# Moving large matmul units between the two layers' steps in a two-layer graph attention kernel

## The chip, the cores and the metric

The kernel runs on one core of a Trainium2 chip. The metric is the device time of one execution in microseconds (us); lower is better. Engines are named as in the profile: PE is TensorE's matmuls and PEld its weight loads, DVE is VectorE, ACT is ScalarE, POOL is GpSimd, and SP is SyncE, which here only issues DMAs.

## The reference

For each of 16 graphs with 1024 nodes and 256 features, two attention layers follow each other. Both use the same adjacency matrix as a mask. Layer 0 has 4 heads of 64, layer 1 has 8 heads of 32 and biases on its projections.

```python
def layer(x, adj, H):                       # D = 256 // H
    h = maximum(layernorm(x), 0)
    q, k, v = heads(h @ Wq), heads(h @ Wk), heads(h @ Wv)
    s = where(adj != 0, q @ k.T / sqrt(D), -inf)
    return x + concat(softmax(s, -1) @ v) @ Wo + bo
x = layer(x, adj, 4)                        # layer 0, for each of the 16 graphs
x = layer(x, adj, 8)                        # layer 1
```

## The kernel before

**Tiles and steps.** A layer of one graph is cut into query halves (`qh`, 512 queries each) and, in each half, two groups of heads (`g`), so four groups a layer. A group runs through the keys in steps. One step computes 4 score blocks of 128 keys x 512 queries (`scores`, L396, into two PSUM tiles `ps` of two banks), masks them on DVE (L412), takes exponentials on ACT (L417) into a tile `p`, and two steps later (`LEAD = 2`) multiplies them with the values (`weigh`, L429, into `po`). A layer-0 step holds 2 heads x 2 key tiles, a group has 4 steps and a graph's layer 0 has 16. A layer-1 step holds 4 heads x 1 key tile, a group has 8 steps and a graph's layer 1 has 32.

**The order.** All 768 steps are in one list that is written out by hand: layer 0 of graph 0, then, for every b from 0 to 14, layer 0 of graph b+1 (16 steps, the first is called a) and layer 1 of graph b (32 steps, the first is called c = a + 16), and last layer 1 of graph 15. This text calls the 48 steps from a(b) on *period b*, and names steps a+0 to a+15 and c+0 to c+31; c+32 is the next period's a. Each engine works off its instructions in the order of the program.

**What hangs on the steps.** `later(i, f)` puts f on step i, behind the step's masks and exponentials. The *large units* are `k`, `q` and `values` (a projection of half a graph: 8, 8 and 16 PE instructions) and `end_half` (the output projection of half a graph, L377, 16 instructions). Each takes one PSUM tile from the same three as the scores. When a large unit is due on an even step, that step's `weigh` is put off and done on the following odd step together with its own (`Stream.run`). So the work goes in *pairs* of an even and an odd step, and a pair without a large unit is a *plain pair*. `turn` transposes a normalized half on PE (8 instructions) into a tile `hT`, of which there are two. For b from 1 on, the inputs of layer 1 of graph b (`mine` in the code) are made in the period itself or just ahead of it, those of layer 0 of graph b+2 (`other`) in c+1 to c+30.

**The softmax's sums.** In layer 1, POOL adds the p tiles of two steps (L530), and three accumulating DMAs of 1 MB a group (L516, POOL's queue) add the pairs' sums; one matmul with ones (`count`, L301) then gives the sums. In layer 0, DVE and POOL add the tiles (`add_tiles`, L438 to L444). `spread` copies the sums on ACT and sends them with 2 or 4 small DMAs on SP to `sums`, so that all lanes hold a part. `invert` takes the reciprocal on DVE (L337), writes it to DRAM (`vd`) and reads it back broadcast (`inv`, 2 or 4 DMAs; SP waits for `vd` to land). `normalize` multiplies `cat`, the group's output, on POOL (L348). `end_group` sets the distances: a group whose last `weigh` is done on step i has them, in layer 1, at i + 8, i + 11 and i + 15, and `end_half` at i + 17. The last group of a layer 1 is `brief` (4, 7, 9, 11) and the groups of graph 15's layer 1 are counted in `pairs`.

**Others.** `put` (ACT, L143) and `second` (DVE, L151, eight operations for a graph) make the mask; layer 1 needs `second`'s form. `norms` hangs statistics (DVE, L173) and the normalization (ACT, L190) on steps. `test` compares a layer's sums with two bounds (L247: two DVE instructions for layer 0, four for layer 1) and multiplies into `chk`, which `verdict` reduces at the end (L737), behind all output DMAs. After the last step `run` works off what is still due.

Of the kernel before, what the change touches and what calls it, by code (L numbers as in the profile page):

```python
# [10 lines left out]
F32 = mybir.dt.float32  # L11
# [7 lines left out]
P = 128  # L19
# [63 lines left out]
def fast_program(ctx, tc, a, w, loads, chk):  # L83
# [4 lines left out]
    x, adj, out = a["x"], a["adj"], a["out"]  # L88
    B, N, E = x.shape
    NT = N // P  # L90
# [3 lines left out]
    adjp = ctx.enter_context(tc.tile_pool(name="adjp", bufs=1))  # L94
# [3 lines left out]
    small = ctx.enter_context(tc.tile_pool(name="small", bufs=2))  # L98
# [173 lines left out]
    class Group:  # L272
# [44 lines left out]
        def spread(self):  # L317

            s = work.tile([P, 512], F32, tag="s", bufs=1, name=f"s_{self.n}")
            nc.scalar.copy(s, self.s)  # L320
            inp, k = self.inp, 2 * self.qh + self.g
            if k == 0:
                inp.sums = small.tile(
                    [P, 4 * self.n_f], F32, tag=f"sums{self.layer}", bufs=1, name=f"sums_{inp.n}"
                )
            self.sn = inp.sums[:, k * self.n_f : (k + 1) * self.n_f]
            lanes = P // self.per
            for r in range(self.per):
                nc.sync.dma_start(
                    self.sn[r * lanes : (r + 1) * lanes, :],  # L330
                    s[r * self.D : r * self.D + 1, :].rearrange("r (c f) -> r c f", f=self.n_f),
                )
# [122 lines left out]
    class Stream:  # L455
# [12 lines left out]
        def later(self, i, f, *args):  # L468
            self.due.setdefault(i, []).append((f, args))
# [84 lines left out]
        def end_group(self, i, gr):  # L554

            if gr.hurry:
                for f in (gr.spread, gr.finish, gr.inp.test):
                    self.later(i, f)
                return

            if gr.layer == 0:
                self.later(i + 4, gr.count_added)
                at = 4, 6, 8, 11
            else:
                at = (8, 11, 15, 17)
                if gr.pairs:
                    at = 2, 5, 7, 9
                elif gr.brief:
                    at = 4, 7, 9, 11
            for k, f in zip(at, (gr.spread, gr.invert, gr.normalize)):  # L570
                self.later(i + k, f)
            if gr.last:

                self.later(i + (7 if gr.layer or gr.inp.b == 0 else 37), gr.inp.test)
            if gr.g == 1:
                self.later(i + at[3], gr.end_half)

# [7 lines left out]
    mask, inp = masks[0], inputs[0][0]  # L585
# [76 lines left out]
    def norms(inp, half, *at):  # L662

        for i, f in zip(at, (inp.stats, inp.stats, inp.norm, inp.norm)):
            later(i, f, half, (0, 1) if i in (at[0], at[2]) else (2, 3))
        later(at[3] + 1, inp.add_bias, half)

    def half_inputs(inp, half, *at):

        for i, f in zip(at, (inp.turn, inp.k, inp.q, inp.values)):  # L670
            later(i, f, half)
# [5 lines left out]
    for t in range(NT):  # L677
        i = 6 + 2 * t
# [8 lines left out]
    for b in range(B - 1):  # L687
        mine, a, c = inputs[1][b], first[b + 1], second[b]
        if b == 0:

            norms(mine, 0, a + 5, a + 6, a + 8, a + 9)
            half_inputs(mine, 0, a + 11, a + 12, a + 14, a + 14)
            norms(mine, 1, a + 13, a + 14, a + 15, c)
            half_inputs(mine, 1, c + 1, c + 3, c + 6, c + 4)
        else:
            norms(mine, 0, a - 20, a - 19, a - 16, a - 15)
            half_inputs(mine, 0, a - 13, a, a + 4, a + 6)
            norms(mine, 1, a - 14, a - 10, a - 8, a - 6)
            half_inputs(mine, 1, a - 1, a + 8, c, a + 10)
        for i, u in zip((2, 4, 6, 8, 10, 11, 12, 14), range(NT)):  # L700
            later(a + i, masks[b].second, u)
        if b + 2 < B:
            other, mask = inputs[0][b + 2], masks[b + 2]
            later(a + 3, open_x, b + 2, 0)
            later(a + 13, open_x, b + 2, 1)
            if b == 0:
                norms(other, 0, a + 14, a + 15, c + 2, c + 3)
                half_inputs(other, 0, c + 5, c + 8, c + 16, c + 18)
                norms(other, 1, c + 3, c + 4, c + 6, c + 7)
                half_inputs(other, 1, c + 11, c + 22, c + 26, c + 30)  # L710
            else:
                norms(other, 0, a + 10, a + 12, a + 13, a + 15)
                half_inputs(other, 0, c + 1, c + 8, c + 16, c + 18)
                norms(other, 1, c, c + 4, c + 5, c + 6)
                half_inputs(other, 1, c + 9, c + 22, c + 26, c + 30)
            for i, t in zip((7, 12, 17, 22, 33, 37, 41, 45), range(NT)):
                later(a + i - 5 + (t > 4), mask.load, t)
                later(a + i - 2, mask.flip, t)
                later(a + i, mask.put, t)
        else:  # L720
            last, e = inputs[1][b + 1], c + 32
            norms(last, 0, c + 5, c + 6, c + 8, c + 9)
            half_inputs(last, 0, c + 11, c + 14, c + 16, c + 20)
            norms(last, 1, c + 13, c + 14, c + 16, c + 17)
            half_inputs(last, 1, c + 19, c + 24, e + 6, e + 4)
            for u in range(NT):
                later(c + 8 + 2 * u, masks[b + 1].second, u)
# [158 lines left out]
def kernel(  # L886
# [28 lines left out]
    with ExitStack() as fast, tc.manual_schedule():  # L915
        fast_program(fast, tc, a, w, loads, chk)
# [61 lines left out]
```

## Time and profile before

| | |
|---|---|
| median of 3 runs | 3368.06 us (3367.02 to 3372.03) |
| profiled execution, its own time | 3370.14 us |
| its span, first to last instruction | 3368.4 us |
| busy share of PE, PEld, DVE, ACT, POOL | 98, 38, 75, 64, 70% |
| granted TensorE clock | 0.989 |
| DMA queues, share of 16 engines | 37.0% from POOL, 13.5% from SP |

The busy time of PE includes waits inside a group of matmuls, since the ends of matmuls are modelled. More can be read from the starts of the score matmuls (L396), of which every step has one group: the distance between the starts of two even steps is what a pair takes. In period 5, which starts at 1153.65 us, the pairs take these times (from the timeline of PE; *L* marks a pair with a large unit):

| pair | us | pair | us | pair | us |
|---|---|---|---|---|---|
| a+0 L | 10.18 | c+0 L | 11.24 | c+16 L | 8.76 |
| a+2 L | 11.07 | c+2 | 4.50 | c+18 L | 8.67 |
| a+4 L | 13.76 | c+4 L | 9.24 | c+20 | 4.50 |
| a+6 L | 11.07 | c+6 | 4.51 | c+22 L | 8.00 |
| a+8 L | 11.91 | c+8 L | 9.33 | c+24 | 5.37 |
| a+10 L | 11.07 | c+10 | 4.50 | c+26 L | 7.69 |
| a+12 L | 11.93 | c+12 L | 8.36 | c+28 | 6.09 |
| a+14 | 7.57 | c+14 | 5.13 | c+30 L | 9.52 |

Pairs differ also by what else they hold: a `turn` (1.03 us of PE) or a `count` (0.9 to 2.7 us). Layer 0's pairs are the same in all of the periods 1 to 13; most of layer 1's are, but c+12, c+26 and c+28 vary.

### The profile page before, as it was taken

To read this page: it belongs to the slowest core of one execution; us is meant where nothing else is said; L and a number is where in the kernel's file an instruction comes from. 1 tells how busy PE (TensorE), PEld (TensorE's weight loads), DVE (VectorE), ACT (ScalarE), POOL (GpSimd) and SP (SyncE) were. 2 spreads that over 40 slices of the span, in tenths; PEclk is the share of its full clock that TensorE was granted. 3 is DMA by queue.
4 is the path that set the end of the run, shared out by engine and by line. 5 is a ranking of instruction groups with operands and counts; after the bars stand their busy time and mean duration, and the time that the engine had idled before them with its cause. 6 is when DMAs were issued, how large, how long until landed. Compare 5 with 4: busy or idle time off the path is not lost.

```text
span 3368.4 us, 44431 instructions
## 1 busy us (share of the span) xinstructions
PE 3293.8 (98%) x16990; PEld 1295.9 (38%) x16990; DVE 2528.6 (75%) x2760; ACT 2170.8 (64%) x2402; POOL 2344.8 (70%) x1244
## 2 busy tenths in 40 slices
PE   8999999999999999999999999999999999999898
PEld 3343433433343343433434333343333433433333
DVE  5777786878767787786877768778687776867876
ACT  6567576675756757576675766757567575675565
POOL 4578585775957759587684866848678585775675
PEclk9999999999999999999999999999999999999899
DMA  7348274472734727356282563826548274470431
GB/s 141 67 76 154 54 132 93 88 148 54 147 74 92 144 51 148 73 115 125 59 149 68 107 123 64 165 56 123 98 83 147 57 133 91 92 138 20 97 67 31
DMA packets 309454, 331.75 MB, mean 98 GB/s; under 512 B 189552, under 2 KB 257392, under 8 KB 290032
## 3 DMA queue, kind: packets, MB, share of 16 engines
q0 software_dynamic: 73824, 224.42, 37.0%
q1 hardware_dynamic: 235408, 104.41, 13.5%
q8 instruction: 135, 2.21, 0.3%
q14 instruction: 87, 0.71, 0.1%
HBM read 119.54 MB, written 17.56 MB: 41 GB/s over the span
## 4 chain that ended last, share of the span: by engine, by line
PE 70%; DMA 9%; POOL 9%; DVE 6%; issue 3%; SPq 2%; ACT 2%; POOLq 0%; DVEq 0%; ACTq 0%
PE ps L396 23%; PE po L429 20%; PE pq L225 9%; PE py L377 7%; POOL p L530 6%; PE pv L262 6%; DVE p L412 4%; PE pz L301 4%; DMA inv<-vd 3%; DMA vd<-vn 2%; DMA p<-p 2%; PE ph L208 1%; SPq L342 1%; ACT p L417 1%; POOL p L516 1%
## 5 line engine op out<-in xcount | busy, mean ns | idle before, releaser
L412 DVE SCALAR_TENSOR_TENSOR p<-mask,ps 128x1024 f32<-128x1024 fp8e4 x1536 | 1791.9, 1214 | 629.9 <-PE ps L396 572.4
L417 ACT ACTIVATE p<-p 128x1024 f32<-128x1024 f32 x1536 | 1610.7, 1056 | 926.4 <-DVE p L412 881.9
L530 POOL TENSOR_TENSOR p<-p,p 128x2048 f32<-128x2048 f32 x255 | 1210.1, 4748 | 154.2 <-PE po L429 135.0
L396 PE MATMUL ps<-qT,kT 32*128 32x512 f32 (+1 forms) x6144 | 1207.7, 636 | 30.8 <-DVE p L412 27.8
L429 PE MATMUL po<-p,v 128*32 128x512 f32 (+1 forms) x6144 | 998.1, 605 | 4.8 <-ACT p L417 4.7
L396 PEld LDWEIGHTS ps<-qT,kT 32*128 32x128 f32 (+1 forms) x6144 | 394.8, 185 | 732.4 <-issue 380.1
L442 POOL TENSOR_TENSOR p<-p 128x1024 f32<-128x1024 f32 x128 | 303.0, 2367 | 319.1 <-DVE p L441 314.0
L429 PEld LDWEIGHTS po<-p,v 128*32 128x32 f32 (+1 forms) x6144 | 229.3, 118 | 698.8 <-issue 477.4
L441 POOL TENSOR_TENSOR p<-p 128x1024 f32<-128x1024 f32 x64 | 155.1, 2423 | 330.2 <-DVE p L438 275.5
L377 PE MATMUL py<-wo,cat 128*128 128x256 f32 x1008 | 246.8, 397 | 11.2 <-POOL cat L348 7.6
L225 PE MATMUL pq<-hT,wk 128*128 128x512 f32 x512 | 238.8, 609 | 1.5 <-ACT hT L209 1.3
L262 PE MATMUL pv<-wv,hT 128*128 128x256 f32 x1024 | 239.3, 387 | 0.0
L225 PE MATMUL pq<-hT,wq 128*128 128x512 f32 x512 | 236.6, 605 | 0.1
L348 POOL TENSOR_TENSOR cat<-cat,inv 128x512 f32<-128x512 f32 x127 | 182.9, 1441 | 65.2 <-DMA inv<-vd 63.4
L377 PEld LDWEIGHTS py<-wo,cat 128*128 128x128 f32 x1008 | 191.4, 196 | 91.2 <-issue 50.4
L262 PEld LDWEIGHTS pv<-wv,hT 128*128 128x128 f32 x1024 | 190.5, 191 | 72.4 <-issue 34.1
L516 POOL DMA_DIRECT2D p<-p x150 | 153.6, 1024 | 45.6 <-POOL p L530 19.3
L301 PE MATMUL pz<-p,ones 128*32 128x512 f32 (+1 forms) x1112 | 172.7, 595 | 0.8 <-ACT s L320 0.8
L151 DVE TENSOR_SCALAR mask<-mask 128x1024 fp8e4<-128x1024 fp8e4 x128 | 172.9, 1351 | 0.0
L143 ACT ACTIVATE mask<-adjT,mhalf 128x1024 fp8e4<-128x1024 bf16 x124 | 140.8, 1136 | 32.1 <-DMA adjT<-adj 32.0
L438 DVE TENSOR_TENSOR p<-p 128x1024 f32<-128x1024 f32 x128 | 155.8, 1217 | 0.0
L444 POOL TENSOR_TENSOR p<-p,p 128x1024 f32<-128x1024 f32 x64 | 151.9, 2373 | 5.0
(50 smaller groups left out, 1632.5 us busy)
## 6 DMA issues: line engine op xcount, KB each, us to landing
p<-p POOLq DMA_DIRECT2D x150, 1024.0 KB, 8.4
adj<-in_adj_dram POOLq DMA_DIRECT2D x128, 256.0 KB, 4.4
x<-bo POOLq DMA_DIRECT2D x64, 512.0 KB, 6.4
x<-in_x_dram SPq DMA_DIRECT2D x32, 512.0 KB, 4.0
inv<-vd SPq DMA_DIRECT2D x128, 128.0 KB, 2.9
inv<-vd SPq DMA_DIRECT2D x252, 64.0 KB, 2.5
out_dram<-x SPq DMA_DIRECT2D x31, 512.0 KB, 3.0
sums<-s SPq DMA_DIRECT2D x384, 2.0 KB, 1.8
```

The costliest lines, as they stand in the source:

```text
L225: nc.tensor.matmul(pq[:, m, :], wt[self.layer][:, c, ts(m, P)], self.hT[half][:, c, :], start=(c == 0), stop=(c == 1),)
L262: nc.tensor.matmul(pv[:, i, :], self.hT[half][:, c, ts(i, P)], w.v[self.layer][:, c, :], start=(c == 0), stop=(c == 1),)
L301: nc.tensor.matmul(self.s[r * self.D : (r + 1) * self.D, :], w.ones[:, : self.D], p[:, r, :], start=start, stop=stop,)
L348: nc.gpsimd.tensor_mul(o, o, self.inv)
L377: nc.tensor.matmul(py[:, i, :], self.half.cat[:, c, ts(i, P)], w.o[self.layer][:, c, :], start=(c == 0), stop=(c == 1),)
L396: nc.tensor.matmul(st.ps[i // 2][:, i % 2, :], gr.inp.kT[r * D : (r + 1) * D, gr.g, ts(kt, P)], gr.inp.qT[gr.qh][r * D : (r + 1) * D, gr.g ...
L412: nc.vector.scalar_tensor_tensor(out=half, in0=gr.mask.m[gr.qh][:, kt, :].unsqueeze(1).to_broadcast([P, 2, 512]), scalar=BIG, in1=st.ps[i] ...
L417: nc.scalar.activation(half, half, AF.Exp, scale=gr.scale)
L429: nc.tensor.matmul(gr.o[r * D : (r + 1) * D, :], gr.inp.v[:, kt, h * D : (h + 1) * D], st.p[:, i, :], start=(kt == 0), stop=(kt == NT - 1),)
L442: nc.gpsimd.tensor_add(a, a, b)
L516: nc.gpsimd.dma_start(one, two, accum_op=ALU.add)
L530: nc.gpsimd.tensor_add(one, one, st.p)
```

## The change

Of the inputs of layer 1 of graph b (b from 1 to 14), three large units leave layer 0's pairs or move on in layer 1's: `k` of half 1 from a+8 to c, `values` of half 1 from a+10 to c+2, and `q` of half 1 from c to c+6. `values` of half 0 goes from a+6 to a+8. The eight `second` operations go from steps a + (2, 4, 6, 8, 10, 11, 12, 14) to a + (0, 2, 4, 6, 8, 10, 12, 13).

For the first three groups of each layer 1 but that of graph 15, `invert` comes at i + 10 instead of i + 11; `spread` and `normalize` stay.

The checks of layer 0 of graph 15 and of layer 1 of graph 14, which came at c+38 and c+40 of period 14 (in layer 1 of graph 15), come behind the last step and behind the checks of graph 15's layer 1. So that layer 1 of graph 14 can keep its `sums` till then, those of graph 15's layer 1 take the place of a tile of the adjacency matrix.

```diff
@@ spread
             if k == 0:
-                inp.sums = small.tile(
-                    [P, 4 * self.n_f], F32, tag=f"sums{self.layer}", bufs=1, name=f"sums_{inp.n}"
+                pool, tag = small, f"sums{self.layer}"
+                if self.layer and inp.b == B - 1:
+                    pool, tag = adjp, "adj"
+                inp.sums = pool.tile(
+                    [P, 4 * self.n_f], F32, tag=tag, bufs=1, name=f"sums_{inp.n}"
                 )
@@ end_group
-                at = (8, 11, 15, 17)
+                at = (8, 10, 15, 17)
@@
             if gr.last:
-                self.later(i + (7 if gr.layer or gr.inp.b == 0 else 37), gr.inp.test)
+                k = 7 if gr.layer or gr.inp.b == 0 else 37
+                self.later(i + k if gr.inp.b + gr.layer < B - 1 else len(self.steps) + 2, gr.inp.test)
@@ the due times, b from 1 on (turn, k, q, values)
-            half_inputs(mine, 0, a - 13, a, a + 4, a + 6)
+            half_inputs(mine, 0, a - 13, a, a + 4, a + 8)
             norms(mine, 1, a - 14, a - 10, a - 8, a - 6)
-            half_inputs(mine, 1, a - 1, a + 8, c, a + 10)
-        for i, u in zip((2, 4, 6, 8, 10, 11, 12, 14), range(NT)):
+            half_inputs(mine, 1, a - 1, c, c + 6, c + 2)
+        for i, u in zip((0, 2, 4, 6, 8, 10, 12, 13), range(NT)):
             later(a + i, masks[b].second, u)
```

## The prediction

> **What bounds the kernel now.** I read the page's busy table first, then TensorE's own timeline over one whole period, then the busy time by stretch, then VectorE's timeline where the change puts something new. Durations are those of the one profiled execution: span 3368.4, its own time 3370.1, which is 2.1 above the median of the runs (3368.06). All figures are us.
>
> ```profile
> PE 3293.8 (98%) x16990; PEld 1295.9 (38%) x16990; DVE 2528.6 (75%) x2760; ACT 2170.8 (64%) x2402; POOL 2344.8 (70%) x1244
> ```
>
> 98% suggests that TensorE is all that counts. The timeline (start, duration, engine, line, operation) of period b = 5 shows two kinds of pairs of steps:
>
> ```profile
> 1211.64 1.99 PE L396 MATMUL ps<-qT,kT 64*128 64x512 f32 x8
> 1213.56 3.72 PE L262 MATMUL pv<-wv,hT 128*128 128x256 f32 x16
> 1217.21 1.99 PE L396 MATMUL ps<-qT,kT 64*128 64x512 f32 x8
> 1219.13 3.65 PE L429 MATMUL po<-p,v 128*64 128x512 f32 x16
> ...
> 1234.64 1.99 PE L396 MATMUL ps<-qT,kT 64*128 64x512 f32 x8
> 1236.56 1.94 PE L429 MATMUL po<-p,v 128*64 128x512 f32 x8
> 1238.42 1.99 PE L396 MATMUL ps<-qT,kT 64*128 64x512 f32 x8
> 1240.34 1.94 PE L429 MATMUL po<-p,v 128*64 128x512 f32 x8
> ...
> 1267.19 1.14 PE L396 MATMUL ps<-qT,kT 32*128 32x512 f32 x8
> 1268.26 1.06 PE L429 MATMUL po<-p,v 128*32 128x512 f32 x8
> 1269.26 1.51 PE L396 MATMUL ps<-qT,kT 32*128 32x512 f32 x8
> 1270.70 1.06 PE L429 MATMUL po<-p,v 128*32 128x512 f32 x8
> ```
>
> The first block is layer 0's pair a+10 with a large unit, 11.07 from start to start; the second is layer 0's plain pair a+14, 7.57. Both are gapless. The third is layer 1's plain pair c+6, 4.51. Its work is 2 x 1.07 + 2 x 0.93 = 4.0 (starts of neighbours in gapless stretches), and its second score group lasts 1.51 where the first takes 1.14: TensorE waits inside it for a PSUM tile. By stretch (window, length, then busy time of PE, PEld, DVE, ACT and POOL with their counts, TensorE's clock, DMA share, GB/s):
>
> ```profile
> 1234.64:1242.21 7.57, 7.57 (x35) 2.34 (x33) 6.52 (x6) 5.13 (x7) 6.42 (x3) 1.00 0.40 104
> 1257.95:1267.19 9.24, 9.14 (x56) 4.31 (x53) 8.24 (x12) 5.70 (x7) 8.90 (x9) 1.00 0.45 87
> 1271.70:1281.03 9.33, 9.33 (x53) 3.62 (x49) 6.38 (x7) 8.26 (x12) 9.33 (x6) 1.00 0.69 137
> ```
>
> The pairs c+4 and c+8, each after a plain pair, take 9.24 and 9.33; the pair c+18, large after large, takes 8.67 with the same sort of content. So layer 0 is TensorE's, and layer 1 alternates: VectorE and POOL fall behind in a plain pair (four mask operations of 1.21 alone are 4.86) and TensorE pays in the next.
>
> **What the Trainium skill says.** "Perfetto Trace Analysis" (Identifying the Most-Contended Engine) warns that matmul busy share is no measure of the distance to the roof; the 1.51 above, booked as busy, agrees. "SBUF — State Buffer" (Who interferes with whom) says that a VectorE instruction with two SBUF inputs and a GpSimd one that reads SBUF exclude each other for the whole instruction. The trace agrees: L247's four checks in the last layer take 6.68 beside POOL's additions, 0.18 to 0.19 each at the very end. "TensorE: Matmul & The Clock Gate" (What's actually happening) says that the clock halves after an idle window of about 3.4; after that 4.98 wait, a `weigh` of 1.06 takes 1.94. "DMA: Bandwidth & Descriptors" (Issuing engines are not separate DMA queues) says that all queues share 16 engines; the sums' transfers land in 1.8 in the median, but 4.3 to 5.3 at c+17 of this period.
>
> **Large units (periods 1 to 14).** k of half 1 goes from a+8 to c, values from a+10 to c+2, q from c to c+6, values of half 0 from a+6 to a+8. Layer 0 loses two large units: pairs a+6 and a+10 fall from 11.07 to 7.57, the value of a+14: 2 x -3.50 = -7.00. What VectorE has there: 4.86 of masks, 1.22 for one addition (the other of these pairs is POOL's, as in a+14), one `second` of 0.7 to 1.7, in a+10 statistics of 1.20: 7 to 9. It exceeds 7.57 only in a+10, and the neighbouring pairs of 11.9 absorb that; if not, +1. In layer 1, c+2 and c+6 become large: 1.07 + 3.65 + 1.07 + 1.85 = 7.64 each for 4.50: +6.28. c+4 and c+8 no longer follow a plain pair: 7.64 + 0.97 (count) = 8.61 and 7.64 + 1.03 (turn) = 8.67, so -0.63 and -0.66. c keeps a unit; the evacuation of 1.37 moves to ScalarE (5.3 of 11.24 are exponentials), q's 1.5 on VectorE falls into a pair of 7.64. Sum -2.01 a period, x14 = **-28** (-35 to -12).
>
> **The wait at c+12.** In three of 13 periods (4, 7, 8) the pair c+12 takes 14.2, 14.0 and 13.1 instead of 8.4: `normalize` waits for `inv`, whose second transfer missed the pause between two accumulating transfers. 16 in all. With q at c+6, the inverse (step c+7) comes after a longer pair and POOL is less behind. I take half, **-8** (-16 to +6).
>
> **Inverses a step sooner (periods 0 to 14).** `spread` stays, so the reciprocal gets one step less behind the sums' four transfers. Here VectorE has:
>
> ```profile
> 1317.62 2.35 DVE L412 SCALAR_TENSOR_TENSOR p<-mask,ps 128x1024 f32<-128x1024 fp8e4 x2 [1.53 <-PE ps L396]
> 1319.89 0.24 DVE L337 RECIPROCAL vn<-sums 128x16 f32<-128x16 f32 x1
> 1320.05 4.55 DVE L412 SCALAR_TENSOR_TENSOR p<-mask,ps 128x1024 f32<-128x1024 fp8e4 x4
> ```
>
> These are c+20's masks, the reciprocal, c+21's. It moves ahead of the first line, in the idle 1.53. But the sums land on average 7.15 after ScalarE's copy (periods 1 to 13, 6.2 to 8.6), the masks start 5.86 after it. With about 0.4 for wait and reciprocal, the masks are 1.7 late, less 0.15 for the reciprocal gone: 1.5, and TensorE, which waits for them there, is too. Behind VectorE are the masks of c+20 and c+21, behind these the k unit's PSUM tile. Against this: `vd` is issued about 0.9 sooner (8.4 to 7.5 after the copy). Now it queues behind the accumulating transfer that POOL issues at 7.5 and lands at 15; ahead of it, `inv` would land some 6 sooner and POOL's wait of 2.5 at `normalize` (c+24) goes, which now delays masks around c+28 (6.09 in the median for a plain pair). SP's queue ahead of `vd` is the same transposing load as before.
> The second group (spread c+25, now c+27 instead of c+28) is the worse one: the reciprocal already stands at the landing (sums land 0.1 to 0.3 before it), so VectorE waits at c+27 with c+28's masks behind it, some 2. For the third group (a+3) the sums land 2.2 ahead of the masks' end: nothing. If `vd` gets ahead (I guess two periods in three), the two groups cost about 0 together, else 2.0, since the first group's delay goes into waits for POOL that are there anyway: 0.8 x 15 = **+12** (-10 to +55).
>
> **Checks.** L1(14)'s four go from step c+40 behind everything. What they hold up now (VectorE, then TensorE):
>
> ```profile
> 3265.97 0.25 DVE L337 RECIPROCAL vn<-sums 128x16 f32<-128x16 f32 x1
> 3266.13 6.68 DVE L247 SCALAR_TENSOR_TENSOR chk<-sums,chk 128x32 f32<-128x32 f32 x4
> ```
> ```profile
> 3274.00 2.08 PE L396 MATMUL ps<-qT,kT 32*128 32x512 f32 x4 [4.98 <-DVE p L412]
> ```
>
> That pair takes 14.60, its neighbours with the same content 5.36: up to -9.2, with the slow clock. At least 5, so **-8**. L0(15)'s two at c+38 took 0.18 and 0.19 beside an idle POOL: nothing. At the end six of about 0.23 make 1.4, in VectorE's gap of 1.76 before the reduction L737, which waits for the output's landing: 0 (at most +1). `sums` in the pool of the adjacency tile: no instruction more.
>
> **`second` earlier.** The same eight operations, 0.7 to 2.1 each; u = 7 moves behind a+13's additions, u = 0 to a, where VectorE is busy 4.9 of 10.2: 0 (-3 to +7). The last batch's own `second` (unmoved) waits 3.3 and 8.4 behind POOL in c+8 to c+13 of period 14, and shifts: 0 (-8 to +8).
>
> **Sum**: -28 - 8 + 12 - 8 = -32: 3370.1 - 32 = 3338, or 3336 from the median. I say 3337.
>
> **Rivals.** (1) *VectorE's wait for the sums decides; slower.* If no `vd` gets ahead and both waits count in full, 1.5 + 2.5 = 4.0 a period, x15 = +60; with -28 for the units and -8 for the checks, +24: 3392 from the median. It decides from (28 + 8 + 8) / 15 = 2.9 a period. For: the landing times. Against: where VectorE waits at c+28 it mostly waits for POOL as well, so the waits overlap. (2) *Layer 0's plain pairs become VectorE's.* If a+6 and a+10 last 8.6, units give -28 + 29 = 0; with the checks and +12, +4: 3372, no change. Against: VectorE's 6.5 busy in a+14, which stays at 7.57 in every period. (3) *All helps*: `vd` always ahead, c+28 falls from 6.8 (mean) to 5: -28 - 16 - 9 - 25 = -78: 3290. For: the chain of waits runs through POOL and `inv` between c+13 and c+29. (4) The units' tiles (hT, kT) are held up by a buffer: each is used last at least three steps before its slot is taken, so I give it nothing.
>
> **How the numbers follow.** Forecast (3318 to 3355) 0.52; rival 1 0.2; rival 2 0.16; rival 3 0.12. 0.2% (6.7) is about what a measurement of this kernel can tell from no change. Faster by more: 0.52 + 0.12 + a quarter of rival 2 = 0.68; within: half of rival 2 and 0.02 of rival 1, 0.1; slower: the rest of both, 0.22. The range takes in the forecast, rival 2, the lower part of rival 1 (its waits partly overlapped, up to +14) and rival 3 down to -56: 3312 to 3382. What is left out is the full rival 1 and the full rival 3.
>
> **What would show it.** Right: a+6 and a+10 at 7.57, c+2 and c+6 at 7.64, c+4 and c+8 at 8.6 to 8.7; fewer long c+12; no L247 before the end; the pair 14.60 at about 5.4. Half wrong: idle time before L337 ended by `sums<-s` (now 8.6 over seven waits) rising to 15 or more. Wrong: a+6 or a+10 over 8, or c+20 to c+31 longer by over 3 a period.

## The result, and the profile after

The kernel after takes **3364.6 us** (median of 12 runs, 3352.2 to 3372.6), the kernel before beside it 3365.7 (12 runs, 3358.9 to 3372.0). The ratio is 0.9994 with an interval of 0.998 to 1.0008: no change that can be told. The prediction had said 3337 and "faster". Its range (3312 to 3382) holds the time; its most probable direction was wrong.

The profiled execution of the kernel after took 3366.5 itself, its span is 3364.7. Its lines are those of before moved by 4 or 5: scores L400, masks L416, exponentials L421, `weigh` L433, `py` L381, reciprocal L341, sums' transfers L333, `normalize` L352. The busy table first:

```profile
PE 3267.3 (97%) x16990; PEld 1277.7 (38%) x16990; DVE 2518.0 (75%) x2760; ACT 2181.5 (65%) x2402; POOL 2347.4 (70%) x1244
```

TensorE is busy for 26.5 us less (3293.8 before) with the same 16990 instructions, but the span is only 3.7 shorter. Busy time includes waits inside a group of matmuls, so with the same instructions the first number says that such waits became less; the second says that TensorE stands idle between its groups for 22.8 us more. TensorE's timeline of period 5 (start, duration, engine, line, operation) shows the gain, in a+10, and one place where it is smaller than forecast, in c+2:

```profile
1223.13 1.99 PE L400 MATMUL ps<-qT,kT 64*128 64x512 f32 x8
1225.05 1.94 PE L433 MATMUL po<-p,v 128*64 128x512 f32 x8
1226.92 1.99 PE L400 MATMUL ps<-qT,kT 64*128 64x512 f32 x8
1228.84 1.94 PE L433 MATMUL po<-p,v 128*64 128x512 f32 x8
...
1260.42 1.09 PE L208 MATMUL ph<-ident,hn 128*128 128x128 f32 x8
1261.44 1.14 PE L400 MATMUL ps<-qT,kT 32*128 32x512 f32 x8
1263.69 3.72 PE L262 MATMUL pv<-wv,hT 128*128 128x256 f32 x16 [1.12 <-ACT hT L209]
1267.35 1.14 PE L400 MATMUL ps<-qT,kT 32*128 32x512 f32 x8
```

a+10 is a plain pair of 7.57 now, gapless (its window is below). In c+2 the values' matmuls wait 1.12 for ScalarE's copy of the transposed tile (L209): the `turn` just ahead (`ph`, L208) had taken one of the three PSUM tiles, and the values need it back. Window by window (length, busy time of PE, PEld, DVE, ACT and POOL with counts, clock, DMA share, GB/s), the pairs a+10, c+2, c+4, c+6 and c+20 are:

```profile
1223.13:1230.70 7.57, 7.57 (x34) 2.35 (x32) 7.33 (x11) 4.03 (x5) 5.91 (x3) 1.00 0.19 35
...
1261.44:1270.27 8.83, 7.71 (x49) 4.00 (x49) 4.10 (x4) 5.76 (x7) 6.79 (x5) 1.00 0.22 30
1270.27:1278.92 8.65, 8.65 (x56) 4.19 (x52) 7.69 (x11) 5.15 (x6) 7.27 (x6) 1.00 0.30 61
1278.92:1286.55 7.63, 7.63 (x42) 2.48 (x40) 5.17 (x6) 6.59 (x10) 5.78 (x4) 1.00 0.44 86
...
1330.24:1338.24 8.00, 6.55 (x33) 1.27 (x32) 4.72 (x5) 4.81 (x5) 8.00 (x3) 0.83 0.96 159
```

The last line is the loss. c+20 took 4.50 before and takes 8.00 here (6.53 in the mean of periods 1 to 13). TensorE is busy for only 6.55 of it and its clock falls to 0.83. VectorE's timeline says what was waited for:

```profile
1327.54 2.35 DVE L416 SCALAR_TENSOR_TENSOR p<-mask,ps 128x1024 f32<-128x1024 fp8e4 x2 [1.20 <-PE ps L400]
1333.51 0.25 DVE L341 RECIPROCAL vn<-sums 128x16 f32<-128x16 f32 x1 [3.61 <-DMA sums<-s]
1333.67 4.55 DVE L416 SCALAR_TENSOR_TENSOR p<-mask,ps 128x1024 f32<-128x1024 fp8e4 x4
```

Before, the reciprocal stood between the masks of c+20 and c+21 and waited for nothing. Now it stands ahead of both and waits 3.61 for the sums to land (to be complete in their tile), with the four masks of the two steps behind it. Over the whole kernel (the table of waits: who waits for what, us in total, times, longest), first of before, then of after:

```profile
POOL cat L348 <- DMA inv<-vd: 63.4, 24, 4.7
...
DVE vn L337 <- DMA sums<-s: 8.6, 7, 4.0
```
```profile
DVE vn L341 <- DMA sums<-s: 88.4, 28, 8.4
...
POOL cat L352 <- DMA inv<-vd: 8.9, 5, 2.9
```

POOL's waits for the inverse are nearly gone (63.4 to 8.9), as the sooner inverse would have it. In their place VectorE waits for the sums, 88.4 in 28 places: 44.5 of it at the first group's reciprocal (ahead of c+20's masks) in 14 periods and 43.9 at the second group's (ahead of c+28's) in 14. At the end of the kernel, the pair that held the checks (14.60 before) and the checks themselves:

```profile
3275.22 1.14 PE L400 MATMUL ps<-qT,kT 32*128 32x512 f32 x8
...
3280.59 1.14 PE L400 MATMUL ps<-qT,kT 32*128 32x512 f32 x8
```
```profile
3354.78 2.22 DVE L247 SCALAR_TENSOR_TENSOR chk<-sums,chk 128x32 f32<-128x32 f32 x10
3357.31 0.18 DVE L742 TENSOR_REDUCE row<-chk 128x1 f32<-128x32 f32 x1 [0.31 <-DMA out_dram<-x]
```

The pair lasts 5.37, and all ten checks fit ahead of the reduction, which still waits 0.31 for the output.

All pairs that differ, mean of periods 1 to 13 (from the starts of the score matmuls):

| pair | before | forecast | after |
|---|---|---|---|
| a+6, a+10 | 11.07 | 7.57 | 7.57 |
| c+2 | 4.51 | 7.64 | **8.83** |
| c+4 | 9.23 | 8.61 | 8.66 |
| c+6 | 4.51 | 7.64 | 7.63 |
| c+8 | 9.34 | 8.67 | 8.65 |
| c+12 | 9.62 | 9.0 | 7.99 |
| c+20 | 4.50 | c+20 to c+30: +0.8 in all | **6.53** |
| c+26 | 7.91 | | 7.70 |
| c+28 | 6.84 | | **7.93** |
| period | 206.13 | 204.3 | 206.64 |

The profiled spans add up so: periods 1 to 13 +0.5 each, +6.5; period 0 (no unit was moved there, only the inverses) 214.2 to 220.7, +6.4; period 14 216.9 to 213.7, -3.2; graph 15's layer 1 with the end 142.8 to 129.4, -13.4. That makes the measured -3.7.

### The profile page after: what moved, and what is told of

Read it like the earlier page. It is cut to its first block, busy times and chain, and to the rows that moved or that the text cites. A ratio compares the mean times of both kernels' runs of the same rounds, so it can differ in the third digit from the quotient of the medians.

```text
span 3364.7 us, 44402 instructions
## 1 busy us (share of the span) xinstructions
PE 3267.3 (97%) x16990; PEld 1277.7 (38%) x16990; DVE 2518.0 (75%) x2760; ACT 2181.5 (65%) x2402; POOL 2347.4 (70%) x1244
## 3 DMA queue, kind: packets, MB, share of 16 engines
q1 hardware_dynamic: 235408, 104.41, 13.8%
## 4 chain that ended last, share of the span: by engine, by line
PE 77%; DMA 7%; ACT 5%; DVE 4%; POOL 3%; issue 2%; SPq 2%; DVEq 0%; ACTq 0%; POOLq 0%
PE ps L400 26%; PE po L433 23%; PE pq L225 11%; PE py L381 7%; PE pv L262 6%; PE pz L301 4%; DVE p L416 3%; DMA sums<-s 3%; DMA p<-p 3%; POOL p L534 3%; ACT p L421 2%; SPq L333 1%; DMA adjT<-adj 1%; ACT mask L143 1%; PE ph L208 1%
## 5 line engine op out<-in xcount | busy, mean ns | idle before, releaser
L421 ACT ACTIVATE p<-p 128x1024 f32<-128x1024 f32 x1536 | 1617.8, 1057 | 938.1 <-DVE p L416 892.4
L416 DVE SCALAR_TENSOR_TENSOR p<-mask,ps 128x1024 f32<-128x1024 fp8e4 x1536 | 1792.0, 1214 | 564.7 <-PE ps L400 547.8
L534 POOL TENSOR_TENSOR p<-p,p 128x2048 f32<-128x2048 f32 x255 | 1190.7, 4672 | 267.0 <-PE po L433 237.5
L400 PE MATMUL ps<-qT,kT 32*128 32x512 f32 (+1 forms) x6144 | 1187.2, 641 | 42.4 <-DVE p L416 40.8
L433 PE MATMUL po<-p,v 128*32 128x512 f32 (+1 forms) x6144 | 1003.0, 608 | 10.9 <-ACT p L421 10.3
L400 PEld LDWEIGHTS ps<-qT,kT 32*128 32x128 f32 (+1 forms) x6144 | 377.2, 186 | 739.0 <-issue 343.6
L446 POOL TENSOR_TENSOR p<-p 128x1024 f32<-128x1024 f32 x128 | 318.7, 2490 | 303.8 <-DVE p L445 298.8
L433 PEld LDWEIGHTS po<-p,v 128*32 128x32 f32 (+1 forms) x6144 | 230.0, 118 | 704.6 <-issue 521.9
L445 POOL TENSOR_TENSOR p<-p 128x1024 f32<-128x1024 f32 x64 | 151.4, 2366 | 263.5 <-DVE vn L341 162.0
L381 PE MATMUL py<-wo,cat 128*128 128x256 f32 x1008 | 236.6, 388 | 2.3 <-ACT hT L209 1.0
L381 PEld LDWEIGHTS py<-wo,cat 128*128 128x128 f32 x1008 | 188.5, 192 | 74.0 <-issue 48.6
L520 POOL DMA_DIRECT2D p<-p x150 | 150.9, 1006 | 40.2 <-POOL p L534 22.2
L352 POOL TENSOR_TENSOR cat<-cat,inv 128x512 f32<-128x512 f32 x127 | 169.2, 1332 | 12.3 <-DMA inv<-vd 8.9
L143 ACT ACTIVATE mask<-adjT,mhalf 128x1024 fp8e4<-128x1024 bf16 x124 | 140.6, 1135 | 28.2 <-DMA adjT<-adj 28.1
L225 PEld LDWEIGHTS pq<-hT,wk 128*128 128x128 f32 x512 | 93.6, 193 | 146.9 <-issue 102.5
```

Of the source, the lines that this page charges most:

```text
L143: nc.scalar.activation(self.m[qh][:, :, ts(t % 4, P)], self.flipped.pop(t), AF.Identity, bias=w.mhalf[:, 0:1], saturate=False,)
L225: nc.tensor.matmul(pq[:, m, :], wt[self.layer][:, c, ts(m, P)], self.hT[half][:, c, :], start=(c == 0), stop=(c == 1),)
L352: nc.gpsimd.tensor_mul(o, o, self.inv)
L381: nc.tensor.matmul(py[:, i, :], self.half.cat[:, c, ts(i, P)], w.o[self.layer][:, c, :], start=(c == 0), stop=(c == 1),)
L400: nc.tensor.matmul(st.ps[i // 2][:, i % 2, :], gr.inp.kT[r * D : (r + 1) * D, gr.g, ts(kt, P)], gr.inp.qT[gr.qh][r * D : (r + 1) * D, gr.g ...
L416: nc.vector.scalar_tensor_tensor(out=half, in0=gr.mask.m[gr.qh][:, kt, :].unsqueeze(1).to_broadcast([P, 2, 512]), scalar=BIG, in1=st.ps[i] ...
```

## The experiments

**Theory A**: units and checks bring what was forecast, and the inverses take it back, by VectorE's wait for the sums. **Rival B**: the units bring less, since the loss at c+20 to c+30 comes from layer 1's new large pairs. Later a **theory D** was added: the sooner inverse makes a collision between transfers. All ratios are to the kernel before on the same chip (medians 3365.6 to 3370.0); a difference between two experiments can be one between two chips.

### Each part by itself

`e1_inverse_back` is the kernel after with its inverses back:
```diff
-                at = (8, 10, 15, 17)
+                at = (8, 11, 15, 17)
```
`e2_inverse_alone` is the kernel before with the opposite edit, `e3_units_alone` the kernel before with only this:
```diff
-            half_inputs(mine, 0, a - 13, a, a + 4, a + 6)
+            half_inputs(mine, 0, a - 13, a, a + 4, a + 8)
-            half_inputs(mine, 1, a - 1, a + 8, c, a + 10)
+            half_inputs(mine, 1, a - 1, c, c + 6, c + 2)
```
and `e4_checks_alone` the kernel before with the last checks behind everything else (the diff's edits to `spread` and to `test`).

> The changed kernel with the inverses at i + 11 again; all else of the change stays. Theory A (the reciprocal, one step sooner, stands before the landing of the sums and holds the masks up): steps c+18 to c+31 fall from 45.0 us a period back to about 42, and period 0 from 220.7 to 214; about 44 us less than the changed kernel, near 3322 us, and 1.3% under the kernel before. Waits of L341 for sums<-s fall from 88 us to about 9. Rival B (the inverse is harmless, the moved units themselves disturb the later steps of layer 1): within 5 us of the changed kernel, near 3363 us, and c+18 to c+31 stay at 45 us.

> The kernel before with the inverses at i + 10 and nothing else. Theory A: about 2.9 us a period more, and 6 us in period 0: near 3405 us, 1.2% over the kernel before. Rival B: within 5 us of the kernel before. Rival C (a sooner inverse helps here because POOL's wait at normalize in c+24 goes, and costs only beside the moved units): 5 to 20 us faster than the kernel before.

> The kernel before with only the large units moved (values of half 0, and k, values and q of half 1). Theory A: a+6 and a+10 at 7.57, c+2 at 8.8, c+6 at 7.63, c+12 without 14 us: about 2.4 us a period less, 14 periods, so some 34 us under the kernel before, near 3332 us. Rival B: no faster than the kernel before, 3360 to 3370 us.

> The kernel before with only the last checks of sums put behind everything. Both theories: the pair of 14.6 us in layer 1 of graph 15 goes to about 5.4 and the end gets no longer: 9 to 11 us less, near 3356 us. Rival: the stall only passes to the next VectorE instruction with two SBUF inputs: no difference.

| kernel | us | ratio to before | waits of VectorE for sums |
|---|---|---|---|
| e1, all but the inverses | 3322.6 | 0.9871 [0.9857, 0.9886] | 13.1 (11) |
| e2, inverses alone | 3406.7 | 1.0122 [1.0106, 1.0137] | 96.7 (28) |
| e3, units alone | 3337.0 | 0.9905 [0.9889, 0.9921] | |
| e4, checks alone | 3357.5 | 0.9973 [0.9963, 0.9983] | |

The parts add up: units -30.2, checks -9.6 and inverses +39.6 against the 3367.1 of before make -0.2, and the whole change measured -1.1. Rival B falls: in e1 the new large pairs are all there and c+20 takes 4.50, c+28 6.92. The inverses cost 42 in the changed kernel (3364.6 less 3322.6) and 40 in the old one, 2.6 to 2.8 in each of 15 periods. Period 0 is 214.2 again in e1.

### The turn out of the values' way

```diff
-                half_inputs(other, 0, c + 1, c + 8, c + 16, c + 18)
+                half_inputs(other, 0, c + 2, c + 8, c + 16, c + 18)
```
in e1, so that `turn` comes behind the values of c+2.

> e1 (the change with the inverses back at i + 11), and the turn of the next graph's half 0 on c+2, behind values, instead of on c+1. If c+2 takes 8.83 instead of 7.64 us because the values' PSUM tile is the one that the transposition of c+1 filled and ScalarE has not yet copied, then c loses 1.03, c+2 takes 8.67 with the transposition in it, and 1.2 us a period go: 15 us under e1, near 3308 us. Rival: ScalarE's lateness in c+1 has another victim at once (weigh waits for the exponentials instead): no difference from e1, 3322 us.

**3308.5**, ratio 0.9829 [0.9806, 0.9852]. TensorE's timeline of c+2 in this kernel:

```profile
1238.21 1.14 PE L400 MATMUL ps<-qT,kT 32*128 32x512 f32 x8
1239.28 3.72 PE L262 MATMUL pv<-wv,hT 128*128 128x256 f32 x16
1242.84 1.04 PE L208 MATMUL ph<-ident,hn 128*128 128x128 f32 x8
1243.80 1.43 PE L400 MATMUL ps<-qT,kT 32*128 32x512 f32 x8
```

The 1.12 ahead of the values is gone, and only 0.3 comes back, inside the next scores: c falls from 11.24 to 10.22, and c+2, which holds the `turn` now, stays at 8.8. Only periods 1 to 13 have this `turn`, and 14 us less were measured, 1.1 each. This version beats both kernels by 1.7%.

### Which inverse, and what its wait is worth

`e6_no_wait_for_sums` is the kernel after with a reciprocal of a constant (it leaves out the division by the sums, and with it the wait for them; all transfers stay); `e7_first_group_sooner` and `e8_second_group_sooner` are the kernel after with i + 10 for one group of a half only; `e12_third_group_sooner` is e5 with i + 10 for the third.
```diff
 e6
-            nc.vector.reciprocal(vn, self.sn)
+            nc.vector.reciprocal(vn, w.ones[:, : self.n_f])
 e7 (e8: (0, 1); e12, on e5: (1, 0))
-                at = (8, 10, 15, 17)
+                at = (8, 10 if (gr.qh, gr.g) == (0, 0) else 11, 15, 17)
```

> The changed kernel (inverses at i + 10) with the reciprocal taken of a constant tile, so that it waits for no transfer of sums; the output's softmax is then not divided by the sums. Spread, the transfers, vd, inv and normalize all stay. Theory A (VectorE standing before the sums' landing is the whole cost): c+18 to c+31 back to 42 us a period or less, 3310 to 3325 us. Rival D (the cost is that vd and inv, issued sooner, collide with the accumulating transfers and the adjacency loads): no faster than 3355 us.

> The changed kernel with i + 10 kept only for the first group of each layer 1 (reciprocal at c+19); the other groups at i + 11. If the costs of the two groups overlap, as the prediction had it, little over e1: c+20 at 6.5 us, but c+28 near 5 us: 3325 to 3332 us. If they add up, some 2 us a period over e1: near 3350 us.

> The changed kernel with i + 10 kept only for the second group (reciprocal at c+27). If the waits at c+27 are the larger cost: c+20 at 4.5 us, c+28 at 8 us or more, 15 to 30 us over e1: 3338 to 3352 us. If they are hidden behind POOL: within 5 us of e1, 3322 us.

> The fastest version so far (inverses at i + 11, turn at c+2; 3308.5) with the inverse of the third group alone (that of a+3) a step sooner. The prediction costed it at nothing, since its sums land 2.2 us before the masks' end: 3308 within 4, no wait for sums at a+2, a+2 and a+4 unchanged at 11.07 and 13.76. Rival: it is a third part of what the sooner inverse costs, +14: 3320 or more.

| kernel | us | ratio to before | us against its base | c+20 | c+28 |
|---|---|---|---|---|---|
| e7, first group | 3341.0 | 0.9929 [0.9909, 0.995] | +18 to e1 | 6.73 | 5.28 |
| e8, second group | 3370.2 | 1.0012 [1.0002, 1.0022] | +48 to e1 | 4.50 | 10.18 |
| after, both and the third | 3364.6 | 0.9994 [0.998, 1.0008] | +42 to e1 | 6.53 | 7.93 |
| e12, third group | 3309.0 | 0.983 [0.9817, 0.9844] | +0.6 to e5 | 4.50 | 6.97 |
| e6, all three, no wait | 3346.2 | 0.9945 [0.9926, 0.9964] | +24 to e1 | 4.50 | 8.88 |

The third group is free, as forecast. The second is the dear one: c+28 takes 3.3 more than in e1, VectorE's waits for sums rise from 13.1 to 44.6 (18 places), and the mean clock falls from 0.993 to 0.984. The first pays 2.2 at c+20 and gets 1.6 back at c+28 in the profiled run (against e1's 4.50 and 6.92); its 14 runs lie far apart, from 3323 to 3365. The two prices do not add (18 and 48, together 42); why not was not settled.

The surprise is e6. Without any wait for the sums the kernel should have been as quick as e1 or quicker; 24 of the 42 stayed, now at c+28.

### What takes the place of the wait

A slab is a tile of 128 rows of the adjacency matrix. POOL's queue loads it (L128), SP's queue transposes it (L134), and ScalarE's `put` makes a part of the mask of it (L143). In e6, ScalarE waits 87.7 us for transposed slabs, in 16 places. Compare c+23 to c+25 of period 5 in e1 and in e6 (SP's queue, POOL, ScalarE):

```profile
1324.33 1.31 SPq L134 DMA_TRANSPOSE adjT<-adj  x1
...
1324.98 1.28 POOL L352 TENSOR_TENSOR cat<-cat,inv 128x512 f32<-128x512 f32 x1 [2.51 <-DMA inv<-vd]
...
1326.20 0.92 POOL L520 DMA_DIRECT2D p<-p  x1
...
1327.40 1.15 ACT L143 ACTIVATE mask<-adjT,mhalf 128x1024 fp8e4<-128x1024 bf16 x1 [1.04 <-DMA adjT<-adj]
```
```profile
1334.48 1.30 POOL L352 TENSOR_TENSOR cat<-cat,inv 128x512 f32<-128x512 f32 x1
1335.71 0.90 POOL L520 DMA_DIRECT2D p<-p  x1
1335.91 1.27 SPq L134 DMA_TRANSPOSE adjT<-adj  x1
...
1344.32 1.15 ACT L143 ACTIVATE mask<-adjT,mhalf 128x1024 fp8e4<-128x1024 bf16 x1 [5.98 <-DMA adjT<-adj]
```

In e1 POOL waits 2.51 for the inverse, so its accumulating transfer of 1 MB (L520) is issued 1.9 *behind* the transposing load, which lands within 3.1. In e6 POOL does not wait, the accumulation is issued 0.2 *ahead*, and the load takes 8.4. POOL's wait had been keeping the accumulation behind the load. From the landings in the traces: the load takes 7.1 to 9.8 in 13 of the 14 periods 0 to 13 of e6, each time issued behind the accumulation; in the one where it is issued ahead it takes 3.1. In e1 it is behind in 2 periods (7.9 and 8.8) and takes 3.0 to 3.6 in the other 12. Behind `put` (L143), ScalarE has `spread`'s copy and the exponentials of c+27.

The kernel after has a part of this as well. There the transposing load is late in periods 2, 3 and 11, and period 2 shows what follows at c+28 (ScalarE, then VectorE):

```profile
730.36 1.15 ACT L143 ACTIVATE mask<-adjT,mhalf 128x1024 fp8e4<-128x1024 bf16 x1 [8.74 <-DMA adjT<-adj]
731.42 0.56 ACT L320 COPY s<-pz 128x512 f32<-128x512 f32 x1
...
735.67 0.25 DVE L341 RECIPROCAL vn<-sums 128x16 f32<-128x16 f32 x1 [8.36 <-DMA sums<-s]
```

`put` stands for the slab, `spread`'s copy comes behind it, so the sums land late, and VectorE waits 8.36 for them. c+28 takes 14.3, 12.7 and 10.0 in these three periods and 6.6 in the mean of the other ten of periods 1 to 13; e1 has 9.4 in its two late periods and 6.5 in the other eleven. So a late load and the wait for the sums can be one chain, and half of the second group's 43.9 us of waits (21.7) stand in three periods.

Five kernels test this, all with the constant in place of the sums. `e10_no_wait_at_eleven` is the control, e1 with the constant; `e14_first_group_no_wait` is e6 with i + 10 for the first group only. The others are e6 with one edit more: `e9_put_later` moves the visible victim, `put`, by two steps; `e13_slab_sooner` loads the slab a step sooner; `e15_slab_own_tile` does that with a tile of its own.
```diff
 e9
-                later(a + i, mask.put, t)
+                later(a + i + 2 * (t == 6), mask.put, t)
 e13, e15
-                later(a + i - 5 + (t > 4), mask.load, t)
+                later(a + i - 5 + (t > 4) - (t == 6), mask.load, t)
 e15
-                at = adjp.tile([P, N], BF16, tag="adj", name=f"adj_{self.b}_{t}")
+                pool, tag = (work, "s") if t == 6 and self.b > 1 else (adjp, "adj")
+                at = pool.tile([P, N], BF16, tag=tag, bufs=1, name=f"adj_{self.b}_{t}")
```

> The kernel with the inverses back at i + 11 (3322.6), and reciprocals of ones (the softmax is not divided by its sums). It is the control for the same edit at i + 10 (3346.2). At i + 11 VectorE waits for the sums only 13.1 us in 11 places, so by the theory that the wait at i + 10 is what the edit takes away, this kernel gains at most 13: 3316 (3309 to 3324), waits of POOL for inv unchanged near 69 us. Rival: the reading of the sums costs something by itself (a slower landing for other transfers), then it gains 20 or more: below 3305.

> The kernel without a wait for the sums (reciprocals of ones, so the softmax is not divided by its sums), with the sooner inverse in the first group alone. If the late transposing load comes from the first group's early end of POOL's wait, it stays in full: waits for adjT 80 us or more, c+28 near 8.5, 3346 (3336 to 3352). If the second group brings it, c+28 is 6 to 7 as at i + 11, and the time 3322 to 3330.

> This is the kernel without a wait for the sums (reciprocals of ones, so the softmax is not divided by its sums), whose time was 3346.2; one more edit: the mask's sixth-index `put` of a period (ScalarE, c+25) stands at c+27, two steps behind its transposing load. Theory D, collision: the inverse that lands sooner lets POOL issue the accumulation of c+25 ahead of or beside the transposing load of c+23, ScalarE stands for that load in `put` (87.7 us in 16 waits) with `spread`'s copy and c+27's exponentials behind it, and c+28 takes 8.9 in the mean where the one period that escaped took 4.6. Then the waits for adjT fall under 45 us, c+28 goes to 4.6 to 6, and the time to 3346 - 15 x 3.5 = 3290 (3280 to 3305). Rival: the load is only where the delay shows and POOL or the shared SBUF port holds c+28: c+28 stays at 8 or more, 3338 to 3350.

> The kernel without a wait for the sums and both inverses at i + 10 (reciprocals of ones, so the softmax is not divided by its sums; 3346.2), with the seventh adjacency slab's load at c+20 instead of c+21. Theory D: the slab then lands some 6 us sooner, the transposing load of c+23 is issued ahead of the accumulation of c+25 and lands in time, and both of its victims (`put` on ScalarE, the next slab's load on POOL) go. POOL itself pays up to 1.4 us at c+20, where it waits for the slab's tile. c+28 falls from 8.9 to 5 or less with c+30 at 9.5: 3346 - 15 x 3 = 3300 (3285 to 3325). Rival: the loss is POOL's and VectorE's shared work and only shifts again: the sum of c+26 to c+31 stays at 25.9 and the time over 3335.

> As the kernel with the seventh slab loaded at c+20 (reciprocals of ones, so the softmax is not divided by its sums; 3362), but that slab lies in the slot of `spread`'s copy `s`, which is idle between c+21 and c+25, so POOL's load need not wait for the slab before. Theory D (the late transposing load is the whole rest): no wait of POOL for adjT at c+20, c+26 back at 7.8, c+28 near 4.5, c+30 at 9.4: 3346 - 15 x 3.5 = 3293 (3280 to 3315). Rival: VectorE and POOL cannot work off these steps sooner, and the loss shows a third time in another pair: 3335 or more, with no wait for adjT left.

| kernel, all without a wait for the sums | us | ratio to before |
|---|---|---|
| e10, i + 11 | 3326.6 | 0.9881 [0.9866, 0.9897] |
| e6, i + 10 | 3346.2 | 0.9945 [0.9926, 0.9964] |
| e14, i + 10 for the first group only | 3347.5 | 0.9954 [0.9937, 0.997] |
| e9, i + 10, `put` later | 3364.6 | 1.0001 [0.9992, 1.0009] |
| e13, i + 10, slab sooner | 3362.5 | 0.9989 [0.9969, 1.001] |
| e15, i + 10, slab sooner in its own tile | 3323.1 | 0.9865 [0.9837, 0.9893] |

e10 and e14 came out as theory D has it: the constant by itself brings nothing, and the first group alone brings the whole of the second loss. Without its wait (e14, 3347.5) that group is no quicker than with it (e7, 3341.0). e9 did not come out so. c+28 fell to 4.50 in nearly every period, but c+30 rose from 9.0 to 14.6. POOL and VectorE of e9 in period 5:

```profile
1345.59 0.61 POOL L128 DMA_DIRECT2D adj<-in_adj_dram  x1 [3.72 <-PE ps L400]
```
```profile
1350.78 4.62 DVE L416 SCALAR_TENSOR_TENSOR p<-mask,ps 128x1024 f32<-128x1024 fp8e4 x4 [3.08 <-POOL p L534]
```

The same late transposition has a second victim: POOL's load of the next slab needs the tile that it reads from. The profile names TensorE as the releaser, but the scores had long been done; by the trace the slab's transposition landed at 1345.0, and in 12 of the 14 periods this load is issued 0.6 behind that landing. e13 took the collision away and made POOL wait at c+20 for the only tile (42.7 us in 16 places over the whole kernel), and c+26 rose by 3. e15, where the slab lies in the idle slot of `spread`'s copy, avoids both; its waits for the slab are

```profile
POOL adj L129 <- DMA adjT<-adj: 6.2, 3, 2.2
...
ACT mask L144 <- DMA adjT<-adj: 4.5, 4, 1.9
```

and its time is that of the control e10. Its transposing load is not quick (6.3 to 11.7), but it is issued sooner: it lands 2.2 to 9.3 after the start of c+24, where e6's 13 late ones land at 13.8 to 15.8. The same edit at i + 11 (e16, below) gains nothing, so what e6 had kept of the price was the late load. The sooner inverse doesn't reach below i + 11 even then: e15 was expected at 3293 and took 3323. c+26 (8.83) holds a new wait of POOL, whose next accumulation waited 3.2 for the one before it in period 5.

### Tried on the fastest version

`e11_turn_and_put` is e5 with e9's edit, `e16_turn_and_slab` e5 with e15's.

> The fastest version so far (inverses at i + 11, turn at c+2; 3308.5) with the `put` of c+25 at c+27. ScalarE waits 37.4 us in 16 places for adjT there; by theory D a part of it is in the way of `spread` and of c+27's exponentials: 3297 (3285 to 3308). Rival: POOL's wait for inv (65 us) sets c+28 with the accumulations of inv's queue, the put is beside it: 3308 within 4.

> The fastest version so far (inverses at i + 11, turn at c+2; 3308.5) with the seventh slab at c+20 in the slot of `s`. ScalarE's 37.4 us of waits for adjT go; c+28 (6.9 in the mean) falls by 1 at most, since POOL waits for inv there anyway: 3300 (3290 to 3311). Rival: the slab's transfer takes the place of inv's, inv lands later and POOL's waits grow: 3312 or more.

3314.7 both (0.9847 [0.9831, 0.9863] and 0.9844 [0.9821, 0.9866]): no better than e5's 3308.5 (the intervals overlap). In e16 POOL's waits for `inv` fell from 64.9 to 38.4 and those for the slab nearly went, without a gain: in these steps a wait that is removed is mostly replaced.

## Why the prediction was wrong, and where it was right

- **What bounds the kernel** held: layer 0's new plain pairs are TensorE's (7.57 in all of the periods 1 to 14, so rival 2 is out, if narrowly: VectorE is busy for 7.33 of a+10), and layer 1's stretch c+20 to c+31 is a chain of VectorE, POOL, ScalarE and transfers.
- **Large units** were forecast at -2.01 a period and, with c+12, at -36. Pairs a+6, a+10, c+4, c+6 and c+8 came within 0.05. c+2 is 1.19 over its 7.64: the sum counted the matmuls of the pair and not the PSUM tile of the `turn` ahead, so the pairs give -0.80 instead of -2.01. c+12 made up for it: no long one is left in periods 1 to 13, -1.63 a period where -0.6 was taken. POOL's waits for `inv` there fell from 11.2 us in three places to 2.2 in one, in e3 as well, which agrees with the reason given; that the two errors cancel is luck. Units alone measured -30 (e3).
- **Checks**: -8 forecast, -9.6 measured (e4). The end tail cost nothing.
- **`second` sooner**: forecast 0. It was not run alone; units and checks taken off leave 3327 (3367.1 - 30 - 10) against e1's 3322.6, so about 4 are left for it, which is inside the intervals.
- **Inverses a step sooner** is the step that failed: +12 (0.8 a period) forecast, +40 to +42 (2.6 to 2.8) measured. Its own odds, one period in three at 2.0, make 0.67 a period and +10; the slip is small. What failed is three terms.
  - The first group's 1.5 was 2.2 at c+20 (e7). What it lacked is, at least in part, the clock. In the kernel after, c+20 takes 5.73 in the eight periods in which the clock stays full, 1.2 over the 4.50 of before, and 7.82 in the other five of periods 1 to 13. The waits are longer in those five as well (3.8 against 2.5), but not by as much: period 9 waits 3.78 at full clock and takes 6.87, period 5 waits 3.61 at 0.83 and takes 8.00.
  - The second group's "some 2" was about 3.3 (c+28 in e8, 10.18 against 6.92).
  - "The two groups cost about 0 together" if `vd` gets ahead was wrong in kind. The first group's `vd` got ahead of the accumulation (landed within 4.2) in 7 of 15 periods, where 10 were guessed, and POOL's waits for `inv` fell from 63.4 to 8.9: what was to pay for the delay did come. But it was worth only 1.6 at c+28 in e7, the second group's wait stood in the same pair and took it, and where no wait for the sums was left the freed POOL ran its transfer into the transposing load (in 13 of 14 periods of e6; in the kernel after in three). A transposing load was named in the prediction only as what stands ahead of `vd` in SP's queue. The trace of before could have shown more: there POOL's wait at `normalize` precedes the accumulation, and the load is issued ahead of it in 12 of 14 periods.
- **Rivals**: the mechanism of rival 1 is in the main what happened, at 2.8 a period instead of its 4.0, just about its own point of decision (2.9). So the kernel ended at no change instead of slower. It had a chance of 0.2; the landing times listed for it deserved more. Rival 4, buffers, got nothing and was right for `hT` and `kT`, which the prediction named, and wrong for PSUM.
- **What would show it** worked: the bound "c+20 to c+31 longer by over 3 a period" was all but reached (+2.9), and "idle before the reciprocal rising to 15 or more" was passed by far (88.4).

## What to carry to other kernels

An instruction that waits on a transfer is not small because it lasts 0.25 us: moved a step ahead on an engine that works in order, it puts the rest of the transfer's latency on everything behind it, so compare its operand's landing with the end of the instruction that it would newly follow. A wait on an engine off the critical path can be what keeps two transfers apart; before removing it, list what that engine issues next and which small transfer would then be behind it. And count PSUM tiles, with the copies that free them, when a matmul unit is moved next to a transpose.

## What the runs showed of the hardware

How long a transfer takes can turn on a few tenths of a microsecond in the order of issue. Of 42 transposing loads of this step (periods 0 to 13 of e1, e6 and the kernel after), the 18 that were issued 0.1 to 1.5 us behind the accumulating DMA of 1 MB took 7.1 to 10.8; the 24 that were issued 0.4 to 6.0 ahead of it took 3.0 to 3.7, but for one (6.0, issued 0.4 ahead). The two are on different queues. Being ahead is not enough by itself: for the 24 the accumulation before had landed, but in e15 ten loads were issued 1.2 to 2.4 ahead of one accumulation and 3.4 to 4.5 behind another that was still under way, and took 6.3 to 11.7.

Waits go together with a lower clock, and the clock is a part of the price. The mean granted clock was 0.993 in e1, 0.985 in e2 and in the kernel after, and 0.83 in the pair c+20 shown above. By these means the lower clock took 50 us of the span of the kernel after (0.015 x 3364.7) and 23 of e1's (0.007 x 3325.0). That is an estimate and an upper bound, since TensorE also stands idle while its clock is low: up to 27 of the 40 us between these two profiles.
